# Projecting B and C of a state-space unit as one pair by seven quarter products

## The chip, the core and the metric

The kernel runs on one core of a Trainium2 chip, as one program in one launch. The metric is the device time in microseconds (us); the figure for a kernel is the median of its runs. All arithmetic is in float32.

The core has five engines, each of which works through its own queue of instructions in order: the Tensor engine (PE; its weight loads are listed apart as PEld), the Vector engine (DVE), the Scalar engine (ACT), the GpSimd engine (POOL) and the Sync engine (SP), which here only issues DMAs. An instruction that has to wait for another engine's result holds up everything behind it in its own queue.

## What is computed

The reference is a two-layer model over an input of 2 x 512 x 512. The change lies in the mixer of the second layer (`_L1_attn_ref`, a Mamba-2 block). Cut to what matters:

```python
proj = jnp.einsum('bsd,od->bso', h, in_proj_w)
gate = proj[..., :D_INNER]
hBC = proj[..., D_INNER:D_INNER + CONV_DIM]
hBC = jax.nn.silu(causal_conv(hBC, conv_w, conv_b))
hid = hBC[..., :D_INNER].reshape(b, s, H_M, P_M)
B = hBC[..., D_INNER:D_INNER + G_M * N_M].reshape(b, s, G_M, N_M)
C = hBC[..., D_INNER + G_M * N_M:].reshape(b, s, G_M, N_M)
...
M = jnp.einsum('bcihn,bcjhn->bcijh', Ch, Bh) * jnp.transpose(L, (0, 2, 3, 4, 1))
Y_diag = jnp.einsum('bcijh,bcjhp->bcihp', M, hc)
...
Y_off = jnp.einsum('bclhn,bchpn,bhcl->bclhp', Ch, prev_states, jnp.exp(A_cs))
y = (Y_diag + Y_off).reshape(b, S, H_M, P_M)[:, :s] + D_res
yg = y * jax.nn.silu(gate)
ygr = ygr * jax.lax.rsqrt(jnp.mean(ygr * ygr, axis=-1, keepdims=True) + EPS)
out = jnp.einsum('bsd,od->bso', y, out_proj_w)
```

Here the model width is 512 (four blocks of 128 rows, `KD` = 4), the sequence is 512 long (`S`; four chunks of 128, `NCH` = 4), there are 128 heads of 64 channels in 8 groups, and each group has one B and one C of 128 states for each of the two batch rows. B and C of one group and row are each the product of a 128 x 512 slice of the weight with the 512 x 512 input `hT`.

## The kernel before, in words

The mixer goes through 16 *units* (`u`), a group and a batch row each (`g, b = divmod(u, 2)`). A unit has 8 tiles of 128 channels, that is two heads each. They are taken two at a time by `step(d)`, so a unit has four steps, which are named by the number `t` of their first tile: t = 0, 2, 4, 6. In every step a pipeline is at work: `a` are the two tiles whose outputs are multiplied now, `n` the next two, whose decays, values and states are made ready, `h` the two after these, whose channels are projected, and `p` the previous two, whose outputs are gated, squared and summed.

Nothing is scheduled by a tool here. The whole stage is under `tc.manual_schedule()`, so each engine's queue has exactly the order in which `step` writes its instructions. Most steps go through the branch `if gates:`; the first unit and parts of the last take the `else` branch.

Names that the change and the prediction touch:

- `Values` and `Gates` project a pair of tiles (256 output columns) by *seven products of quarters*: the two factors are cut into quarters, sums of quarters are made beforehand (of the weight's by `row_sums`, four POOL instructions at L691; of the input's once, in `th`), and seven products in place of eight give the result after a few additions. `multiply(i)` writes product i; `product` (L717) is two matmuls over 128 rows with 256 columns. Products 1, 6, 7, 4 gather in one half of a PSUM bank, and in between its state is copied out by ACT (`copy`, L1464 and L1509) and added on by DVE (`add` and `add_fifth`, L1469, L1473, L1513).
- `project` (L1249) is the plain product: four matmuls over 128 rows with 512 columns.
- `inner(u, j)` projects B (j = 0) or C (j = 1) of a unit by `project` into the PSUM bank `of` (profile name `pjbc`). In step t = 0 of a unit it is done for the unit after it (`projected = u + 1`).
- `conv` is `first_tap` (ACT, L1259) and `taps` (three DVE instructions, L1268, each using the result of the one before). It is used for the channels (`hid`), for B (`BT`) and for C (`CT`).
- `clamp` (ACT, L1364, four instructions) and `decays` (an exponential on ACT into the single PSUM bank `de`, L1378, then a DVE product with `CB`, L1379) make the decay matrix of one head; there are two heads a tile, so four of these in each step.
- `values` (DVE, L1350) reads the transposed channels `px` (PE, L1340); `begun` (PE, `pn`, L1386), an ACT copy (L1395) and four DVE instructions (L1399) make the states `st`.
- `finish_y` (DVE, L1315 and L1316) takes a product `py` of the tiles `a` out of PSUM. `starts` (POOL, L1411) multiplies C into the decay tile `eb` that a DMA has brought.
- `square` (ACT, L1328) and its `add` (POOL, L1332) gather the squares of a unit; `squares` (PE, `ssq`, L1840) sums them over the partitions at the end of step t = 0 of the next unit. `root` (ACT with a table load, L1828) and a DVE reciprocal (L1829) follow in step t = 2.
- `Output` multiplies a finished unit by the output weights, again in seven products (`of`, `ofy`, L1640), in the steps t = 2, 4, 6 of the next unit; `added` is the DVE addition of a product to the result (L1663). The sums of quarters of y that it needs are made by POOL (L1608) into three rooms with the tags `s1`, `s2`, `s4`. In step t = 0 there is no output work.
- PSUM banks: `pj` has three buffers, `yy` two, `of`, `de` and `tr` one each.

In step t = 0 the order of the B and C work on PE was: products 1, 5, 2, 3 of the channels, then all of B, then the transposes of the second tile, the channels' product 6, and so on; C came in two halves of two matmuls, each between two products of the gates.

Of the kernel before, what the change touches and what calls it, by code (L numbers as in the profile page):

```python
# [8 lines left out]
F32 = mybir.dt.float32  # L9
# [6 lines left out]
P = 128  # L16
D = 512
B = 2
# [30 lines left out]
def fused_kernel(  # L49
# [1110 lines left out]
    with ExitStack() as sm:  # L1160
# [83 lines left out]
            sls[g] = wk.tile([P, 4, NT, GH], F32, tag="sl", name=f"sl{g}")  # L1244
            nc.sync.dma_start(sls[g], sl_d[g])

        def project(w_of, b, ps, ks=range(KD)):
            for k in ks:
                nc.tensor.matmul(  # L1249
                    ps, w_of(k), hT[:, k, bass.ts(b, S)], start=(k == 0), stop=(k == KD - 1)  # L1250
                )
# [84 lines left out]
        def transposed(s, spare=False):  # L1336
            tag, bufs = ("pj", 3) if spare else ("tr", 1)
            px = psum.tile([P, NCH, P], F32, tag=tag, name=f"px{s}", bufs=bufs)
            for c in range(NCH):
                nc.tensor.transpose(px[:, c, :], hid[s][:, bass.ts(c, P)], ident)  # L1340
            return px
# [67 lines left out]
        def starts(s):  # L1409

            nc.gpsimd.tensor_tensor(  # L1411
                eb_t[s],
                CTs[s // GT][:, P:].unsqueeze(1).to_broadcast([P, 2, S - P]),
                eb_t[s],
                ALU.mult,
            )
# [110 lines left out]
            project(lambda k: whs[s // 2][:, k, bass.ts(s % 2, P)], b, ps)  # L1527
            return ps, g * GT + t, hid[s]

        def inner(u, j, parts=False):  # L1530

            g, b = divmod(u, B)
            kept, name = ((BTs, "BT"), (CTs, "CT"))[j]
            kept[u] = wk.tile([P, S], F32, tag=name, name=f"{name}{u}", bufs=j + 1)
            if u == 0 and j == 1:
                ps = psum.tile([P, S], F32, tag="yy", name=f"pjbc{u}_{j}", bufs=2)
            else:
                ps = psum.tile([P, S], F32, tag="of", name=f"pjbc{u}_{j}")

            def go(ks):  # L1540
                project(lambda k: wbc[g][:, k, j, :], b, ps, ks)
                return ps, DIN // P + j * NG + g, kept[u]

            return go if parts else go(range(KD))

        def inner_products(u):

# [19 lines left out]
        class Output:  # L1567
# [18 lines left out]
            def banks(self, p):  # L1586

                return ("of", 1), ("yy", 2)
# [166 lines left out]
        def step(d):  # L1755
# [38 lines left out]
                    load_final(2 + i, sums_room(1, i))  # L1794


            for s in p:
                nc.gpsimd.tensor_tensor(y_of(s), y_of(s), sgs.pop(s), ALU.mult)  # L1798
            gates = ahead.pop(d, None)
            made = (g == 0 and b == 0 and t == 2) or (0 < g < NG and b == 1 and t == 0)  # L1800
            if (d - 1) in rest_of_sums:
                sum_out(g, 1)
# [51 lines left out]
            if gates:  # L1854

                def output(n=1):
                    if o:
                        o.multiply(n)

                def added():  # L1860
                    if o:
                        o.add()

                late = t == 2
                px = transposed(n[0])
                hids.multiply(1, 5)
                hcd = [values(n[0], px)]
                decays(n[0], 0)
                hids.copy(0, 0)
                hids.multiply(2, 3)  # L1870
                hids.add(0, 0)
                decays(n[0], 1)
                starts(n[0])
                output()
                if projected is not None:
                    b_of = inner(projected, 0)
                px = transposed(n[1])
                hids.multiply(6)
                if not late:
                    added()  # L1880
                hcd.append(values(n[1], px))
                decays(n[1], 0)
                if projected is not None:
                    conv(*b_of)
                hids.copy(0, 1)
                gates.multiply(1, 5)
                decays(n[1], 1)
                starts(n[1])
                if t == 4 and o:
                    o.sums(1)  # L1890
                hids.multiply(7)
                hids.copy(1, 1)
                gates.copy(0, 0)
                root()
                gates.multiply(2)
                pn = begun(n[0], hcd[0])
                hids.multiply(4)
                states(n[0], pn)
                if late:
                    added()  # L1900
                for f in [square(s) for s in p]:
                    f()
                hids.add_fifth()
                hids.add(0, 1)
                hids.add(1, 1)
                gates.multiply(6)
                output()
                if projected is not None:
                    c_of = inner(projected, 1, True)
                    c_of(range(0, KD // 2))  # L1910
                gates.copy(0, 1)
                convolved = hids.sum(0)
                first_tap(*convolved)
                if not late:
                    taps(*convolved, added)
                first_sums()
                gates.multiply(7)
                first_tap(*hids.sum(1))
                gates.copy(1, 1)

                def gates_added():
                    gates.add(0, 0)
                    gates.add(1, 1)

                if late:

                    def between():
                        added()
                        gates_added()


                    taps(*convolved, between)
                else:
                    gates_added()
                output()
                added()
                if projected is not None:
                    c_of = c_of(range(KD // 2, KD))
                pn = begun(n[1], hcd[1])
                gates.multiply(4)  # L1940
                taps(*hids.sum(1))
                output()
                added()
                states(n[1], pn)
                if projected is not None:
                    first_tap(*c_of)
                pss = squares()
                gates.multiply(3)
                silu()
                gates.add(0, 1)  # L1950
                output(int(t < 6))
                gates.silu()
                mean(pss)
                added()
                if projected is not None:

                    taps(*c_of)
# [206 lines left out]
```

## Time and profile before

| quantity | us |
|---|---|
| median of 3 runs | 2204.86 |
| lowest and highest run | 2204.32, 2205.11 |
| the profiled execution | 2207.44 |
| its span, first to last instruction | 2205.7 |
| a unit, from the first `py` product of one to that of the next (units 1 to 14) | 104.03 |
| of it the steps t = 0, 2, 4, 6 | 25.42, 26.52, 27.52, 24.57 |

The profile is of one execution. In a timeline row the columns are the start and the duration in us, the engine, the line of the kernel, the operation, what it writes and reads, the shapes and how many instructions are merged in the row; a bracket tells how long the engine was idle before it and what ended the wait. A matmul in float32 is two passes, so two matmuls are x4 there. Because matmuls overlap, the cost of a product is read from the start of its row to the start of the next, not from its duration. The granted clock of the Tensor engine is 0.996 over the span.

### The profile page before, as it was taken

How to read it: one execution, taken by the hardware profiler on the slowest of the kernel's cores; microseconds unless marked ns; L12 is line 12 of the kernel's file. 1: busy time of each engine (PE TensorE's matmuls, PEld its weight loads, DVE VectorE, ACT ScalarE, POOL GpSimd, SP SyncE). 2: the span in 40 equal slices, each digit the busy share in tenths (PEclk: the TensorE clock that was granted, in tenths of full speed). 3: DMA queues.
4: the chain of work that ended last, by engine and by line, in shares of the span. 5: the costliest groups of instructions: out<-in, count | busy, mean ns of one | idle time of the engine just before them, and what ended most of it. 6: DMA issues, size and time to landing. Idle time of an engine off the chain costs nothing.

```text
span 2205.7 us, 35586 instructions
## 1 busy us (share of the span) xinstructions
PE 2180.5 (99%) x12460; PEld 1704.9 (77%) x12460; DVE 1534.4 (70%) x3035; ACT 1295.2 (59%) x2878; POOL 1336.8 (61%) x1275
## 2 busy tenths in 40 slices
PE   8999999999999999999999999999999999999999
PEld 4545566865578888888888888888888888888877
DVE  6474577545877777777777677777777677777762
ACT  4231323215776767676767676767667676767661
POOL 4362532232556667766866586768567776766577
PEclk9999999999999999999999999999999999999999
DMA  5021466756544545443545554454446444544552
GB/s 169 20 77 38 139 220 214 253 171 208 169 144 131 156 139 173 125 134 125 179 137 153 158 154 125 134 163 130 145 140 193 132 137 125 167 126 139 150 177 93
DMA packets 196151, 323.21 MB, mean 147 GB/s; under 512 B 17795, under 2 KB 130180, under 8 KB 193540
## 3 DMA queue, kind: packets, MB, share of 16 engines
q1 hardware_dynamic: 189572, 299.95, 44.8%
q0 software_dynamic: 6400, 20.98, 2.5%
q8 instruction: 99, 1.62, 0.3%
q14 instruction: 80, 0.66, 0.1%
HBM read 294.12 MB, written 26.74 MB: 145 GB/s over the span
## 4 chain that ended last, share of the span: by engine, by line
PE 93%; DVE 3%; DMA 1%; ACT 1%; POOL 1%; issue 0%; SPq 0%; DVEq 0%; ACTq 0%; POOLq 0%
PE pjh L717 16%; PE of L1640 15%; PE gt L717 13%; PE py L1287 5%; PE pjbc L1249 5%; PE pf L1128 4%; PE py L1296 4%; PE pn L1386 4%; PE px L1340 3%; PE ofy L1640 3%; PE pg L717 2%; PE pu L717 2%; PE gty L717 2%; PE sh L610 2%; PE gt L1249 2%; PE pjh L1249 1%
## 5 line engine op out<-in xcount | busy, mean ns | idle before, releaser
L1411 POOL TENSOR_TENSOR eb<-CT,eb 128x768 f32<-128x768 f32 x128 | 230.4, 1820 | 350.1 <-DMA eb<-ea_d 317.4
L1364 ACT ACTIVATE cs<-cs,sl 128x128 f32<-128x128 f32 x1024 | 325.0, 390 | 0.6 <-DMA cs<-cs_d 0.6
L1268 DVE SCALAR_TENSOR_TENSOR hid<-pjh,cw,hid 128x511 f32<-128x511 f32 (+2 forms) x384 | 286.6, 747 | 42.0 <-ACT hid L1259 34.5
L1379 DVE TENSOR_TENSOR cs<-de,CB 128x512 f32<-128x512 f32 x256 | 175.5, 685 | 79.0 <-ACT de L1378 78.1
L1798 POOL TENSOR_TENSOR y<-y,sgt 128x512 f32<-128x512 f32 x124 | 177.0, 1447 | 12.7 <-ACT sgt L1520 10.1
L1287 PE MATMUL py<-cs,hc 128*64 128x128 f32 x2048 | 181.5, 277 | 0.0
L1332 POOL TENSOR_TENSOR sums<-sums,sq 128x512 f32<-128x512 f32 x110 | 139.8, 1271 | 60.0 <-ACT sq L1328 56.3
L1378 ACT ACTIVATE de<-cs 128x512 f32<-128x512 f32 x256 | 154.0, 602 | 30.5 <-DVE cs L1379 24.6
L1296 PE MATMUL py<-eb,st 128*64 128x128 f32 x1536 | 149.9, 274 | 0.0
L1399 DVE SCALAR_TENSOR_TENSOR st<-st,sl,pn 128x64 f32<-128x64 f32 x512 | 108.4, 275 | 59.4 <-ACT st L1395 59.4
L1663 DVE SCALAR_TENSOR_TENSOR acc<-of,rg,acc 128x256 f32<-128x256 f32 x188 | 90.2, 481 | 75.1 <-PE of L1640 74.8
L1464 ACT COPY hid<-pjh 128x256 f32<-128x256 f32 x171 | 63.6, 372 | 133.1 <-PE pjh L717 131.2
L1316 DVE SCALAR_TENSOR_TENSOR y<-hid,Dcol,y 128x512 f32<-128x512 f32 x128 | 135.7, 1060 | 4.5
L1287 PEld LDWEIGHTS py<-cs,hc 128*64 128x64 f32 x2048 | 122.5, 138 | 19.9 <-issue 18.1
L1315 DVE TENSOR_TENSOR y<-py,el 128x512 f32<-128x512 f32 x128 | 87.7, 685 | 58.5 <-PE py L1296 57.7
L1395 ACT COPY st<-pn 128x128 f32<-128x128 f32 x128 | 33.0, 263 | 153.3 <-PE pn L1386 153.3
L1640 PE MATMUL of<-wt,y 128*128 128x256 f32 x512 | 121.8, 381 | 0.0
L1249 PE MATMUL pjbc<-hT,wbc 128*128 128x512 f32 x256 | 119.5, 602 | 1.4 <-DVE g L1138 0.8
L1386 PEld LDWEIGHTS pn<-hcd,Bs 128*128 128x128 f32 x768 | 105.5, 192 | 18.5 <-issue 13.0
L1640 PE MATMUL of<-wo,s 128*128 128x256 f32 x496 | 118.8, 382 | 0.0
L717 PE MATMUL pjh<-th,sh 128*128 128x256 f32 x456 | 117.2, 379 | 0.0
L717 PE MATMUL pjh<-th,wh 128*128 128x256 f32 x456 | 117.2, 379 | 0.0
(389 smaller groups left out, 5534.0 us busy)
## 6 DMA issues: line engine op xcount, KB each, us to landing
cs<-cs_d SPq DMA_DIRECT2D x128, 512.0 KB, 4.3
eb<-ea_d SPq DMA_DIRECT2D x256, 192.0 KB, 6.1
wh<-in_in_wT SPq DMA_DIRECT2D x64, 512.0 KB, 9.2
wg<-in_in_wT SPq DMA_DIRECT2D x64, 512.0 KB, 7.5
el<-ea_d SPq DMA_DIRECT2D x256, 128.0 KB, 7.5
wo<-wo_d SPq DMA_DIRECT2D x16, 1024.0 KB, 8.3
wop<-in_out_wT SPq DMA_DIRECT2D x39, 256.0 KB, 2.8
wo_d<-wop POOLq DMA_DIRECT2D x39, 256.0 KB, 2.7
```

The source lines that it names most:

```text
L717: nc.tensor.matmul(ps, x[:, k, :], y[:, k, :], start=(first and k == 0), stop=(k == 1), skip_group_check=True,)
L1249: nc.tensor.matmul(ps, w_of(k), hT[:, k, bass.ts(b, S)], start=(k == 0), stop=(k == KD - 1))
L1268: nc.vector.scalar_tensor_tensor(dst[:, j:], ps[:, : S - j], cw[:, ct, KCONV - 1 - j : KCONV - j], dst[:, j:], ALU.mult, ALU.add,)
L1287: nc.tensor.matmul(py[bass.ts(hh, HP), bass.ts(c, P)], hc[:, c, bass.ts(hh, HP)], M[:, hh, bass.ts(c, P)], start=True, stop=(c == 0),)
L1296: nc.tensor.matmul(py[bass.ts(hh, HP), bass.ts(c, P)], st[:, c - 1, bass.ts(hh, HP)], cte[:, hh, bass.ts(c - 1, P)], start=False, stop=True,)
L1364: nc.scalar.activation(m[:, bass.ts(c, P)], m[:, bass.ts(c, P)], AF.Relu, bias=sls[g][:, 3, b * NCH + c, h0 + hh : h0 + hh + 1], scale=-1.0,)
L1378: nc.scalar.activation(pe, m, AF.Exp, scale=-1.0)
L1379: nc.vector.tensor_tensor(m, pe, CBs[s // GT].rearrange("p c i -> p (c i)"), ALU.mult)
L1386: nc.tensor.matmul(pn[:, c, :], Bss[s // GT][:, c, :], hcd[:, c, :], start=True, stop=True)
L1411: nc.gpsimd.tensor_tensor(eb_t[s], CTs[s // GT][:, P:].unsqueeze(1).to_broadcast([P, 2, S - P]), eb_t[s], ALU.mult,)
L1640: nc.tensor.matmul(ps, x[:, k, :], y[:, k, :], start=(first and k == 0), stop=(k == 3), skip_group_check=True,)
L1798: nc.gpsimd.tensor_tensor(y_of(s), y_of(s), sgs.pop(s), ALU.mult)
```

## The change

B and C of a unit are now projected together as a pair, like the channels, by seven products. A new class `Inner` does it:

```diff
+        class Inner:
+            def __init__(self, u):
+                self.u = u
+                self.g, self.b = divmod(u, B)
+                w = wbc[self.g].rearrange("p k j o -> p k (j o)")
+                room = [
+                    wk.tile([P, 4, P], F32, tag=f"s{i}", name=f"s{i}_bc{u}", bufs=1) for i in (1, 2, 4)
+                ]
+                s = [r[:, 2 * j : 2 * j + 2] for r in room[:2] for j in range(2)]
+                row_sums(w, *s)
+                self.factors = seven(w, s, hT[:, :, bass.ts(self.b, S)], self.b)
...
+            def banks(self):
+                self.ps = [
+                    psum.tile([P, 2, HD], F32, tag=tag, name=f"pjbc{self.u}_{j}", bufs=bufs)
+                    for j, (tag, bufs) in enumerate((("yy", 2), ("of", 1)))
+                ]
+            def multiply(self, *which):
+                for i in which:
+                    ps = self.ps[int(i not in (2, 3))][:, int(i in (3, 5))]
+                    product(ps, self.factors[i], i in (1, 2))
```

with `copy` (ACT), `add` and `add_fifth` (DVE) as in `Values`. The sums of the weight's quarters lie in the rooms `s1` and `s2` of the output's sums; B gathers in a `yy` bank, C in `of`. In step t = 0:

```diff
+            gates = ahead.pop(d, None)
+            if gates and projected is not None:
+                bc = Inner(projected)
             for s in p:
                 nc.gpsimd.tensor_tensor(y_of(s), y_of(s), sgs.pop(s), ALU.mult)
...
                 px = transposed(n[0])
+                if projected is not None:
+                    bc.banks()
+                    bc.multiply(1, 5)
+                    hids.multiply(1, 5)
+                    hcd = [values(n[0], px)]
+                    decays(n[0], 0)
+                    bc.copy(0, 0)
+                    bc.multiply(2, 3)
+                    clamp(n[0], 1)
+                    hids.copy(0, 0)
+                    bc.multiply(6)
+                    hids.multiply(2, 3)
+                    decays(n[0], 1, True)
+                    bc.add(0, 0)
+                    clamp(n[1], 0)
+                    bc.copy(0, 1)
+                    decays(n[1], 0, True)
+                    bc.add_fifth()
+                    bc.add(0, 1)
+                    first_tap(*bc.sum(0))
+                    hids.add(0, 0)
+                    starts(n[0])
+                    px = transposed(n[1])
+                    hids.multiply(6)
+                    hcd.append(values(n[1], px))
+                    taps(*bc.sum(0))
...
                 if projected is not None:
-                    c_of = inner(projected, 1, True)
-                    c_of(range(0, KD // 2))
+                    bc.multiply(7)
                 gates.copy(0, 1)
                 convolved = hids.sum(0)
                 first_tap(*convolved)
-                if not late:
+                if projected is not None:
+                    bc.copy(1, 1)
+                if not apart:
                     taps(*convolved, added)
                 first_sums()
                 gates.multiply(7)
...
+                if projected is not None:
+                    pn = begun(n[1], hcd[1])
+                    bc.multiply(4)
+                if apart:
                     def between():
                         added()
                         gates_added()
+                        if projected is not None:
+                            bc.add(1, 1)
                     taps(*convolved, between)
                 else:
                     gates_added()
...
-                if projected is not None:
-                    c_of = c_of(range(KD // 2, KD))
-                pn = begun(n[1], hcd[1])
+                if projected is None:
+                    pn = begun(n[1], hcd[1])
+                pss = squares()
                 gates.multiply(4)
...
                 if projected is not None:
-                    first_tap(*c_of)
-                pss = squares()
+                    first_tap(*bc.sum(1))
```

(`apart` is `late or projected is not None`, `late` is t = 2.) So in step t = 0 the additions of the gates, which stood behind all three taps of the first tile, now stand between its first and second tap; the three taps of B stand behind `values` of the second tile instead of behind its first decay; the sum of squares on PE stands ahead of the gates' product 4 instead of behind it; the POOL sums of the weight's quarters stand ahead of the gating of the previous two tiles. The first unit's own B and C, and those of unit 1, are still made by `inner`; the new way is taken in 14 steps, those with t = 0 of units 1 to 14. In steps t = 2, 4, 6 the order of the instructions is as before.

More of the change, by code (lines that the diff above doesn't have):

```diff
@@ L1245, in load_slice, with project @@
             nc.sync.dma_start(sls[g], sl_d[g])
-        def project(w_of, b, ps, ks=range(KD)):
-            for k in ks:
+        def project(w_of, b, ps):
+            for k in range(KD):
                 nc.tensor.matmul(
@@ L1528, in channels, with inner @@
             return ps, g * GT + t, hid[s]
-        def inner(u, j, parts=False):
+        def inner(u, j):
             g, b = divmod(u, B)
@@ L1538, in inner, with quarter, copy, add @@
                 ps = psum.tile([P, S], F32, tag="of", name=f"pjbc{u}_{j}")
[L1540 to L1544, printed above, removed]
+            project(lambda k: wbc[g][:, k, j, :], b, ps)
+            return ps, DIN // P + j * NG + g, kept[u]
+        class Inner:
[9 more added lines that the diff above has]
+                self.factors = seven(w, s, hT[:, :, bass.ts(self.b, S)], self.b)
+                self.kept = []
+                for j, (kept, name) in enumerate(((BTs, "BT"), (CTs, "CT"))):
+                    kept[u] = wk.tile([P, S], F32, tag=name, name=f"{name}{u}", bufs=j + 1)
+                    self.kept.append(kept[u])
+            def banks(self):
[7 more added lines that the diff above has]
+                    product(ps, self.factors[i], i in (1, 2))
+            def quarter(self, i, j):
+                return self.kept[i][:, bass.ts(j, HD)]
+            def copy(self, i, j):
+                nc.scalar.copy(self.quarter(i, j), self.ps[1][:, 0])
+            def add(self, i, j):
+                q = self.ps[i][:, j]
+                nc.vector.tensor_tensor(q, q, self.quarter(i, j), ALU.add)
+            def add_fifth(self):
+                q = self.quarter(0, 1)
+                nc.vector.tensor_tensor(q, self.ps[1][:, 1], q, ALU.add)
+            def sum(self, j):
+                ps = self.ps[j].rearrange("p i n -> p (i n)")
+                return ps, DIN // P + j * NG + self.g, self.kept[j]
         def inner_products(u):
@@ L1794, in step @@
                     load_final(2 + i, sums_room(1, i))
+            gates = ahead.pop(d, None)
+            if gates and projected is not None:
+                bc = Inner(projected)
             for s in p:
                 nc.gpsimd.tensor_tensor(y_of(s), y_of(s), sgs.pop(s), ALU.mult)
-            gates = ahead.pop(d, None)
             made = (g == 0 and b == 0 and t == 2) or (0 < g < NG and b == 1 and t == 0)
@@ L1864, in step @@
                 late = t == 2
+                apart = late or projected is not None
                 px = transposed(n[0])
[L1866 to L1874, printed above, removed]
-                if projected is not None:
-                    b_of = inner(projected, 0)
@@ L1877, in step @@
-                px = transposed(n[1])
-                hids.multiply(6)
-                if not late:
-                    added()
-                hcd.append(values(n[1], px))
-                decays(n[1], 0)
-                if projected is not None:
-                    conv(*b_of)
+                if projected is not None:
+                    bc.banks()
[23 more added lines that the diff above has]
+                    taps(*bc.sum(0))
+                else:
+                    hids.multiply(1, 5)
+                    hcd = [values(n[0], px)]
+                    decays(n[0], 0)
+                    hids.copy(0, 0)
+                    hids.multiply(2, 3)
+                    hids.add(0, 0)
+                    decays(n[0], 1)
+                    starts(n[0])
+                    output()
+                    px = transposed(n[1])
+                    hids.multiply(6)
+                    if not late:
+                        added()
+                    hcd.append(values(n[1], px))
+                    decays(n[1], 0)
@@ L1913, in step @@
                 first_tap(*convolved)
-                if not late:
+                if projected is not None:
+                    bc.copy(1, 1)
+                if not apart:
                     taps(*convolved, added)
@@ L1923, in gates_added @@
                     gates.add(1, 1)
-                if late:
+                if projected is not None:
+                    pn = begun(n[1], hcd[1])
+                    bc.multiply(4)
+                if apart:
                     def between():
@@ L1936, in step @@
                 added()
-                if projected is not None:
-                    c_of = c_of(range(KD // 2, KD))
-                pn = begun(n[1], hcd[1])
+                if projected is None:
+                    pn = begun(n[1], hcd[1])
+                pss = squares()
                 gates.multiply(4)
@@ L1955, in step @@
                 if projected is not None:
-                    taps(*c_of)
+                    taps(*bc.sum(1))
             else:
```

## The prediction

> **What bounds the kernel now.** I read the page's busy times first, then the busy time by stretches for the four steps of one unit, then the timelines of steps t = 0 and t = 2, each engine alone.
>
> ```profile
> span 2205.7 us, 35586 instructions
> PE 2180.5 (99%) x12460; PEld 1704.9 (77%) x12460; DVE 1534.4 (70%) x3035; ACT 1295.2 (59%) x2878; POOL 1336.8 (61%) x1275
> ```
> ```profile
> 942.03:967.45 25.42, 25.42 (x157) 19.65 (x156) 19.31 (x39) 17.66 (x40) 15.11 (x14) 1.00 0.47 135
> 967.46:993.98 26.52, 26.52 (x174) 23.15 (x173) 21.17 (x43) 21.21 (x48) 20.36 (x20) 1.00 0.49 150
> ```
>
> After the stretch and its length stand PE, PEld, DVE, ACT, POOL, granted clock, DMA share and GB/s. PE never rests: its matmuls follow one another through both steps of unit 4 at full clock, so a matmul less should be time less. But step t = 2 is the fullest for all four engines, and there the other queues run just in time. This is the step that the change doesn't edit, and the one that I think decides.
>
> Step t = 0, rows of ACT, PE, POOL and DVE:
>
> ```profile
> 947.66 0.37 ACT L1464 COPY hid<-pjh 128x256 f32<-128x256 f32 x1 [0.49 <-PE pjh L717]
> 948.33 1.03 PE L717 MATMUL pjh<-hT,sh 128*128 128x256 f32 x4
> 949.19 3.60 PE L1249 MATMUL pjbc<-hT,wbc 128*128 128x512 f32 x8
> 952.21 3.59 POOL L1411 TENSOR_TENSOR eb<-CT,eb 128x768 f32<-128x768 f32 x2 [3.75 <-DMA eb<-ea_d]
> 952.62 0.60 PE L1340 MATMUL px<-ident,hid 128*128 128x128 f32 x4
> 958.54 0.86 DVE L1399 SCALAR_TENSOR_TENSOR st<-st,sl,pn 128x64 f32<-128x64 f32 x4 [0.71 <-ACT st L1395]
> 961.06 2.32 DVE L1268 SCALAR_TENSOR_TENSOR hid<-pjh,cw,hid 128x511 f32<-128x511 f32 x3 [0.53 <-ACT hid L1259]
> 963.29 0.41 DVE L1513 TENSOR_TENSOR sgt<-sgt,gty 128x256 f32<-128x256 f32 x1
> 963.62 0.41 DVE L1513 TENSOR_TENSOR sgt<-sgt,gt 128x256 f32<-128x256 f32 x1
> 967.56 0.42 DVE L1513 TENSOR_TENSOR sgt<-sgt,gt 128x256 f32<-128x256 f32 x1 [0.54 <-PE gt L717]
> ```
>
> Step t = 2, rows of the same unit:
>
> ```profile
> 975.75 0.60 ACT L1378 ACTIVATE de<-cs 128x512 f32<-128x512 f32 x1 [1.11 <-DVE cs L1379]
> 979.68 0.60 ACT L1378 ACTIVATE de<-cs 128x512 f32<-128x512 f32 x1
> 980.43 0.37 ACT L1464 COPY hid<-pjh 128x256 f32<-128x256 f32 x1
> 982.63 0.18 DVE L1829 RECIPROCAL rg<-rg 128x4 f32<-128x4 f32 x1 [1.62 <-ACT rg L1828]
> 988.48 1.03 PE L717 MATMUL gt<-th,wg 128*128 128x256 f32 x4
> 988.84 0.48 DVE L1663 SCALAR_TENSOR_TENSOR acc<-of,rg,acc 128x256 f32<-128x256 f32 x1
> 989.37 1.99 PE L1640 MATMUL of<-wo,s 128*128 128x256 f32 x8
> ```
>
> The reader is to see the last two: the DVE addition ends at 988.84 + 0.48 = 989.32 and the output product behind it starts at 989.37. A product takes 0.863 to the next (948.33 to 949.19), so PE was free for it at 988.48 + 0.86 = 989.34. PE already arrives at this wait with nothing in hand.
>
> **What the change takes from PE.** The whole projection of B costs 952.62 - 949.19 = 3.43; C's two halves, from start to next start in the same timeline, 1.71 each. Together 6.86. Seven products at 0.863 are 6.04. The gain is 0.82 a unit, over 14 units 11.5 us. Moving `begun` and the sum of squares on PE changes their place and not their cost.
>
> **What it adds elsewhere.** ACT: three copies at 0.37 (row 947.66), 1.1 us; the first two replace waits for PE of 0.49 and more early in the step. DVE: four additions, 0.33 each start to start (963.29 to 963.62); three come before the middle of the step, where DVE sat idle 2.70 us for the transposes of the second tile, and cost nothing because of that idle time; without it they would cost 1.0. The fourth, for C, stands late, in a queue with no idle time, and costs its 0.33. POOL: four sums over 128 x 256, at 0.73 (the rows of `sh`), 2.92. They stand ahead of the gating, which ends 2.9 later, but the next POOL instruction waits for a DMA anyway: 3.75 idle in unit 4, 8.91 in unit 5. So nothing; if a DMA came sooner, they would cost up to 2.92 at the sum of squares, which waits for POOL's additions. Product 5 of the pair waits for the first sum: POOL turns from the gates' sums to the gating at 945.06 now, 3.03 after the step's start, so the first sum is there at 3.8; PE comes to product 5 one product after 945.74, at 4.6. No DMA is added or moved on a queue, and the PSUM bank `yy` that B takes was read by `finish_y` over 4 us before.
>
> **What it makes late.** In the old order one whole B (3.43) stood ahead of `begun` of the first tile; now products 1, 5, 2, 3, 6 of the pair do, 5 x 0.863 = 4.32. So `begun` comes 0.89 later, and with it the DVE states (958.54), three additions, ACT's first tap and the taps at 961.06. Behind these DVE has the same work as before plus the new addition (0.33), and a wait of about 0.13: the gates' additions now stand right behind the first tap and need ACT's copy, which comes behind two first taps and the new copy of C (0.68 + 0.27 + 0.68 + 0.37 after the start of the first of them; DVE's tap starts 0.83 after that, and DVE is free 1.08 later). Before, DVE waited 0.54 for PE at 967.56; that wait is used up. Sum: 0.89 + 0.33 + 0.13 - 0.54 = 0.81. DVE enters step t = 2 some 0.81 us later, while PE enters it 0.82 us earlier. The lag grows by 1.6.
>
> **Where the lag ends.** From 967.56 DVE works without a gap to the decay product that ACT waits for at 975.75 (1.11 idle). That exponential starts 0.81 later, and ACT goes through clamp, exponential, copy, clamp and exponential back to back until the one at 979.68, whose successor could start at 979.68 + 0.54 = 980.22. The copy at 980.43 waits for PE, so ACT has 0.21 in hand in unit 4. In unit 5 it has 0.47 (an exponential at 1083.45, the copy at 1084.46). PE is early, so this wait of ACT vanishes, and the copy comes 0.81 - 0.21 = 0.60 later than now in even units, 0.34 in odd ones. From there on I find no idle time up to 989.37: gate copy, table load, root, reciprocal (982.63), states, addition, three additions, first tap, taps, addition, output product. So PE's wait ends 0.60 and 0.34 later than it does now, and the rest of the step follows. PE's 0.82 are lost in standing still on the way, 1.42 and 1.16 a unit in step t = 2. In steps t = 4 and 6 PE's rows come from the same order; at the end of t = 2 DVE idles 1.05, so the lag ends there.
>
> **A term that I can't read off.** `finish_y`'s second instruction (L1316) takes 0.75 alone, longer when a POOL row meets it:
>
> ```profile
> 970.91 1.40 DVE L1316 SCALAR_TENSOR_TENSOR y<-hid,Dcol,y 128x512 f32<-128x512 f32 x1
> 972.95 1.04 DVE L1316 SCALAR_TENSOR_TENSOR y<-hid,Dcol,y 128x512 f32<-128x512 f32 x1
> 1074.94 0.84 DVE L1316 SCALAR_TENSOR_TENSOR y<-hid,Dcol,y 128x512 f32<-128x512 f32 x1
> 1076.42 1.30 DVE L1316 SCALAR_TENSOR_TENSOR y<-hid,Dcol,y 128x512 f32<-128x512 f32 x1
> ```
>
> The first two are unit 4's, the others unit 5's. Each ends about 0.55 after the POOL row that it met. Placed again by that, 0.8 later beside POOL rows that in even units shift with PE and in odd units stay (they hang on a DMA), the pair sums to 2.45 in even units (2.44 now) and to 1.95 in odd ones (2.14 now). So odd units lose 0.34 - 0.19 = 0.15. The ends: both alone, 1.50, or both as long as the worst in a step t = 0 or 2, 2.80. Even units then lie between 0.60 - 0.94 and 0.60 + 0.36, odd ones between 0.34 - 0.64 and 0.34 + 0.66: over 7 + 7 units -4.5 to +13.7 us.
>
> **The sum.** 7 x 0.60 + 7 x 0.15 = 5.3 us more. The profiled execution's span goes from 2205.7 to 2211.0; the median lies 0.8 below that span (2204.86), so I forecast 2210.
>
> The Trainium skill's "Perfetto Trace Analysis", section "Identifying the Most-Contended Engine", says to optimize the engine with the highest occupancy first. That is PE here, and by it alone the sum would be 2204.9 - 11.5 = 2193.4. The rows at 988.84 and 989.37 speak against it for this step.
>
> **Rivals.** (1) The gain is kept: the lag is absorbed ahead of the output product, and each unit saves its 0.82: 2193.4. For it: PE is 99% busy and DVE has 6 us of idle time in step t = 0. Against: that idle time lies ahead of `begun`, and the late part of the queue has none. It decides if DVE's lag stays under ACT's slack of 0.2 to 0.5. 0.13. (2) Give and take are about equal: L1316 meets POOL less, and the loss is near the gain: 2200.5 to 2209.2. 0.33. (3) A new stall inside step t = 0. The nearest are the sum of squares in odd units, where POOL's additions end at 1067.58 and PE would come at about 1067.96, 21.9 into a step of 24.6 (0.38 in hand, all hanging on a DMA), and the gates' product 7, whose start now comes two products, 1.73, behind that of product 6, while the copy that it waits for ends 1.07 + 0.37 = 1.44 behind it (958.91 and 959.98 now): 0.29 in hand. From the point where these are used up, each 0.5 us costs 7 us over 14 units: 2217 and more. 0.10. (4) The change doing less than it says: two of 16 units keep the old way, and that is in the sum.
>
> **How the numbers follow.** The forecast's own case, the gain lost and 0.3 to 0.9 more a unit on average, is 2209.2 to 2217, with a chance of 0.44. A difference under 0.2% (4.4 us) can't be told from no change here. Slower by more: this case and (3), 0.54. Within: (2), 0.33. Faster: (1), 0.13. The range takes in the low end of the L1316 bound and stops short of (1) and of most of (3): 2200 to 2216.
>
> **What would show it.** Right: in step t = 0 the pair's seven products in 6.0 and a step of 24.6; in step t = 2 PE idle or stretched by 1.0 to 1.5 us, mostly ahead of the transposes of the second tile, the channels' product 7 and the second-half output products, released by DVE L1350, ACT L1464 and DVE's addition; steps t = 4 and 6 at 27.5 and 24.6. Wrong: a step t = 2 still of 26.5 (then it is 2193), or PE waiting inside step t = 0.

## The result, and the profile after

The median rose from 2204.59 us to 2220.18 us: ratio 1.0074, 95% interval 1.0063 to 1.0085. The change made the kernel slower by 15.6 us. The forecast was 2210 with a range up to 2216; direction and place were right, the size was too small.

The busy times of the page of after, then the two steps of unit 4 by stretches (columns as before), then PE's waits (us in total, times, the longest):

```profile
span 2221.6 us, 36048 instructions
PE 2179.6 (98%) x12628; PEld 1737.3 (78%) x12628; DVE 1553.0 (70%) x3091; ACT 1305.9 (59%) x2920; POOL 1378.4 (62%) x1331
```
```profile
943.27:967.87 24.60, 24.60 (x170) 21.93 (x169) 18.81 (x37) 18.02 (x42) 17.95 (x18) 1.00 0.49 139
967.87:996.34 28.47, 27.11 (x173) 22.99 (x173) 23.39 (x50) 21.63 (x49) 20.33 (x20) 1.00 0.47 140
```
```profile
PE px L1340 <- DVE hcd L1350: 10.5, 12, 1.2
...
PE of L1683 <- DVE acc L1706: 5.1, 14, 0.4
```

The step that was edited is shorter, 24.60 against 25.42: PE has its 0.82 there, and it doesn't wait. The step behind it, with no edit, grew from 26.52 to 28.47, and PE rests in it (27.11 busy). PE's two new kinds of wait both end on DVE. The steps t = 4 and 6 stayed at 27.52 and 24.57. Units 1 to 14 together went from 1456.4 to 1471.0, so 14.6 of the 15.9 us between the two spans lie there: 1.13 in each even unit, 0.95 in an odd one on average.

DVE at the end of step t = 0 of unit 4, with the PE row of the pair's product 4 (it starts at 964.29):

```profile
960.67 0.86 DVE L1399 SCALAR_TENSOR_TENSOR st<-st,sl,pn 128x64 f32<-128x64 f32 x4 [0.85 <-ACT st L1395]
963.18 0.75 DVE L1268 SCALAR_TENSOR_TENSOR hid<-pjh,cw,hid 128x511 f32<-128x511 f32 x1 [0.53 <-ACT hid L1259]
963.85 0.41 DVE L1513 TENSOR_TENSOR sgt<-sgt,gty 128x256 f32<-128x256 f32 x1
964.46 0.42 DVE L1513 TENSOR_TENSOR sgt<-sgt,gt 128x256 f32<-128x256 f32 x1 [0.20 <-ACT sgt L1509]
965.36 0.43 DVE L1579 TENSOR_TENSOR pjbc<-pjbc,CT 128x256 f32<-128x256 f32 x1 [0.48 <-PE pjbc L717]
965.70 3.74 DVE L1268 SCALAR_TENSOR_TENSOR hid<-pjh,cw,hid 128x510 f32<-128x510 f32 x5
970.12 0.41 DVE L1513 TENSOR_TENSOR sgt<-sgt,gt 128x256 f32<-128x256 f32 x1
964.29 1.03 PE L717 MATMUL pjbc<-th,wbc 128*128 128x256 f32 x4
```

The new addition for C (L1579) is not only 0.33 of work: it waits 0.48 for product 4, which ends at 964.29 + 1.03 = 965.32. In the program product 4 is written ahead of the addition, and both touch the bank `of`, product 4 its first half and the addition its second, so the addition waits. The last gates' addition starts at 970.12, 26.85 into the step; before it was 967.56, 25.53 into a longer step. DVE is 1.32 late, not the 0.81 of the forecast.

Step t = 2 of the same unit:

```profile
978.35 0.60 ACT L1378 ACTIVATE de<-cs 128x512 f32<-128x512 f32 x1 [1.81 <-DVE cs L1379]
977.80 0.63 PE L1340 MATMUL px<-ident,hid 128*128 128x128 f32 x4 [0.89 <-DVE hcd L1350]
980.00 1.03 PE L717 MATMUL gt<-th,sw 128*128 128x256 f32 x4
981.13 1.13 PE L717 MATMUL pjh<-th,wh 128*128 128x256 f32 x4
990.35 1.03 PE L717 MATMUL gt<-th,wg 128*128 128x256 f32 x4
991.74 1.99 PE L1683 MATMUL of<-wo,s 128*128 128x256 f32 x8 [0.36 <-DVE acc L1706]
```

The lag surfaces where the forecast had put it: at the transposes of the second tile (0.89), at the channels' product 7 (981.13 - 980.00 is 1.13 where a product takes 0.86), and at the second-half output product (1.39 behind the gates' product; before, 0.89). Together 0.89 + 0.27 + 0.50 = 1.66 of the 1.95 by which the step grew. The other 0.29 is lost right at these waits: from start to start the first costs 1.06, and the products behind the first and the second start 0.02 and 0.10 later than they did.

### The profile page after: what moved, and what is told of

It is laid out like the page before. It is cut to its first block, busy times and chain, and to the rows that moved or that the text cites. A ratio compares the mean times of both kernels' runs of the same rounds, so it can differ in the third digit from the quotient of the medians.

```text
span 2221.6 us, 36048 instructions
## 1 busy us (share of the span) xinstructions
PE 2179.6 (98%) x12628; PEld 1737.3 (78%) x12628; DVE 1553.0 (70%) x3091; ACT 1305.9 (59%) x2920; POOL 1378.4 (62%) x1331
## 3 DMA queue, kind: packets, MB, share of 16 engines
q8 instruction: 100, 1.64, 0.3%
## 4 chain that ended last, share of the span: by engine, by line
PE 77%; DVE 13%; ACT 6%; issue 2%; DMA 1%; POOL 1%; SPq 0%; ACTq 0%; POOLq 0%; DVEq 0%
PE of L1683 13%; PE pjh L717 12%; PE gt L717 9%; PE py L1287 4%; PE pf L1128 4%; PE pjbc L717 4%; DVE hid L1268 4%; PE py L1296 3%; PE pn L1386 3%; PE pg L717 2%; PE pu L717 2%; PE px L1340 2%; PE gt L1249 2%; PE gty L717 2%; PE pjh L1249 2%
## 5 line engine op out<-in xcount | busy, mean ns | idle before, releaser
L1844 POOL TENSOR_TENSOR y<-y,sgt 128x512 f32<-128x512 f32 x124 | 161.4, 1323 | 21.6 <-ACT sgt L1520 18.9
L1316 DVE SCALAR_TENSOR_TENSOR y<-hid,Dcol,y 128x512 f32<-128x512 f32 x128 | 135.0, 1055 | 4.5
L717 PE MATMUL gt<-th,wg 128*128 128x256 f32 x456 | 118.3, 382 | 0.0
L717 PE MATMUL pjh<-hT,wh 128*128 128x256 f32 x456 | 117.1, 379 | 0.0
L717 PE MATMUL gt<-th,sw 128*128 128x256 f32 x456 | 117.0, 379 | 0.0
```

The source lines that it names most:

```text
L717: nc.tensor.matmul(ps, x[:, k, :], y[:, k, :], start=(first and k == 0), stop=(k == 1), skip_group_check=True,)
L1316: nc.vector.scalar_tensor_tensor(y, hid.pop(s), Dcol[:, ct : ct + 1], y, ALU.mult, ALU.add)
```

## The experiments

Nine kernels. The theories are named in the expectations: W, DVE's lag into t = 2 is what PE pays for, and the wait on product 4 is the missed part of it; P, the 0.89 of `begun`, or PE and its banks; X, L1316 against POOL. The steps are means over the seven even and seven odd units of the profiled execution; a ratio is to the runs of before that were made beside that kernel's.

| run | median us | ratio to before (95%) | t = 0 even, odd | t = 2 even, odd | units 1 to 14 |
|---|---|---|---|---|---|
| before | 2204.59 | | 25.42, 25.42 | 26.52, 26.52 | 1456.4 |
| after | 2220.18 | 1.0074 (1.0063 to 1.0085) | 24.60, 24.69 | 28.47, 28.21 | 1471.0 |
| c_addition_later | 2216.75 | 1.0046 (1.0032 to 1.0060) | 24.60, 24.60 | 28.30, 27.75 | 1466.0 |
| begun_early | 2230.09 | 1.0110 (1.0096 to 1.0124) | 25.20, 25.20 | 28.47, 28.23 | 1478.9 |
| both_and_gates | 2205.53 | 0.9995 (0.9984 to 1.0006) | 25.31, 25.31 | 26.52, 26.53 | 1454.9 |
| before_dve_late | 2228.30 | 1.0100 (1.0087 to 1.0114) | 25.42, 25.42 | 28.25, 28.05 | 1479.3 |
| all_and_pe_order | 2197.29 | 0.9959 (0.9944 to 0.9973) | 24.74, 24.74 | 26.51, 26.52 | 1446.8 |
| begun_early_2 | 2224.38 | 1.0081 (1.0067 to 1.0095) | 24.60, 24.75 | 28.47, 28.44 | 1473.1 |
| c_addition_first | 2214.85 | 1.0037 (1.0024 to 1.0049) | 24.86, 24.98 | 27.87, 27.43 | 1465.2 |
| before_dve_late_1 | 2205.53 (one run) | | 25.42, 25.42 | 26.52, 26.53 | 1456.6 |
| all_and_act_order | 2192.82 | 0.9945 (0.9932 to 0.9957) | 24.64, 24.65 | 26.52, 26.52 | 1445.6 |

**before_dve_late: lag without the change.** Before, with DVE work that nothing reads:

```diff
                 gates.add(0, 1)
+                if projected is not None:
+                    spare = wk.tile([P, 4, P], F32, tag="s4", name=f"spare{u}", bufs=1)
+                    spare = spare.rearrange("p k o -> p (k o)")[:, 0:HD]
+                    for _ in range(4):
+                        nc.vector.tensor_tensor(spare, gates.quarter(0, 1), gates.ps[:, 1], ALU.add)
```

> Before with four DVE additions more (the form of the gates' additions, 128 x 256 out of PSUM, written to a room that nothing reads) right behind the last gates' addition of t = 0, in 15 units. PE, ACT and POOL as before. It puts 4 x 0.33 = 1.32 of lag on DVE, the measure that after has. Theory W: PE's step t = 0 stays at 25.4, t = 2 grows by 1.32 - 0.21 = 1.1 in even units and by up to 1.32 - 0.47 = 0.85 in odd ones, 27.6 and 27.4; 14 units give 13.7: 2218. Theory P (PE or its banks, and not DVE's lag, make t = 2 long in after): little, 2205 to 2208.

Nothing of the pair is in this kernel, and yet t = 2 grows from 26.5 to 28.2, with PE's waits at the same instructions as in after. Stretches and two PE rows of unit 4's step t = 2:

```profile
967.62:995.83 28.21, 27.11 (x173) 23.01 (x173) 22.96 (x47) 21.15 (x48) 20.29 (x20) 1.00 0.49 141
```
```profile
977.29 0.63 PE L1340 MATMUL px<-ident,hid 128*128 128x128 f32 x4 [0.62 <-DVE hcd L1350]
991.23 1.99 PE L1640 MATMUL of<-wo,s 128*128 128x256 f32 x8 [0.37 <-DVE acc L1663]
```

So DVE's lag alone is enough to make what after shows; PE's banks or the pair's products are not needed for it. The size was missed because the four additions took 0.45 each and not 0.33: C's taps ended 1.82 later. ACT's second exponential in t = 2 came 1.93 later in unit 4 and the step lost 1.69, so ACT had 0.24 in hand there (0.21 in the forecast).

**before_dve_late_1: one such addition.**

> Before with one DVE addition more behind the last gates' addition of t = 0, in place of four. The four took 0.45 each, start to start, and DVE came 1.82 later into t = 2, where the even units lost 1.69. Theory W with a slack of ACT of 0.21: lag 0.46, L1316 as before, even units' t = 2 at 26.52 + 0.46 - 0.21 = 26.77; odd ones, with 0.47 in hand, at 26.5. A straight line without slack: 26.52 + 0.46 x 1.69 / 1.82 = 26.95 in even units.

Nothing was lost in even units, against both forms of the expectation. C's taps end 0.45 later, but the first L1316 behind them, DVE and then POOL's gating of the same unit:

```profile
969.11 0.96 DVE L1316 SCALAR_TENSOR_TENSOR y<-hid,Dcol,y 128x512 f32<-128x512 f32 x1
970.71 1.05 DVE L1316 SCALAR_TENSOR_TENSOR y<-hid,Dcol,y 128x512 f32<-128x512 f32 x1
968.23 2.98 POOL L1798 TENSOR_TENSOR y<-y,sgt 128x512 f32<-128x512 f32 x2
```

It took 0.96 where it took 1.40 before, and ended 4.88 into the step (4.85 before). L1316 ends with a POOL row, not 0.75 after its own start: the second one ends at 971.76, POOL's gating at 971.21, 0.55 earlier. So a small lag is swallowed here, as long as L1316 meets the same POOL row as before and is longer than the 0.75 that it takes alone.

**c_addition_later: the wait on product 4 taken away on DVE.** From here on every kernel is after with an edit.

```diff
                         gates_added()
-                        if projected is not None:
-                            bc.add(1, 1)
                     taps(*convolved, between)
+                    if projected is not None:
+                        bc.add(1, 1)
```

> After with one DVE instruction moved: the addition for C stands behind all three taps of the channels' first tile instead of between the first and the second. In the profile of after it waits 0.48 us for product 4 of the pair, which fills the other half of the same bank. Theory W (DVE is late into t = 2, and this wait is the part that the forecast missed): the wait goes, DVE's last gates' addition starts 26.85 - 0.48 = 26.4 us into the step t = 0, t = 2 of even units takes 28.47 - 0.48 = 28.0, and 14 units give 6.7: 2213.5. Theory P (the loss comes from begun being late by 0.89, or from PE and its banks): the addition waits or not, t = 2 stays at 28.5, 2220. Theory X (L1316 meets POOL longer): no step change, within 2 us of 2220, and the L1316 pair changes.

The addition no longer waits and DVE's last gates' addition starts at 26.28, as W says. But even units' t = 2 got only 0.17 of it. C's addition now ends 0.87 later than in after, and with it ACT's first tap of C; so the silus behind that on ACT, and POOL's gating, gain little, and L1316 ends with the gating:

```profile
971.19 1.83 DVE L1316 SCALAR_TENSOR_TENSOR y<-hid,Dcol,y 128x512 f32<-128x512 f32 x1
969.98 2.50 POOL L1844 TENSOR_TENSOR y<-y,sgt 128x512 f32<-128x512 f32 x2 [0.73 <-ACT sgt L1520]
```

POOL ends at 972.48, L1316 at 973.02. The same rows of after, and the gating of before:

```profile
973.46 1.44 DVE L1316 SCALAR_TENSOR_TENSOR y<-hid,Dcol,y 128x512 f32<-128x512 f32 x1
971.85 2.50 POOL L1844 TENSOR_TENSOR y<-y,sgt 128x512 f32<-128x512 f32 x2 [0.91 <-ACT sgt L1520]
970.49 2.95 POOL L1798 TENSOR_TENSOR y<-y,sgt 128x512 f32<-128x512 f32 x2
```

Counted from the start of t = 0, DVE's end of C's taps came 0.57 earlier than in after, POOL's gating only 0.16.

The same count shows what happened in after itself. The gating starts there at 28.58 and before at 28.46, so it hardly moved, while DVE's end of C's taps came 1.31 later. The first L1316 slid from the first gating instruction, behind which it ends 0.55 later in before, to the second: 971.85 + 2.50 = 974.35, and L1316 ends at 974.90. In unit 4 of c_addition_later and of c_addition_first, with 0.75 and 0.76 of DVE's lag left, it still ends behind the second; in before_dve_late_1, with 0.46, behind the first. That is why a part of the lag, taken out alone, gave back so little here.

**c_addition_first: the same wait turned round.** DVE's order stays as in after; product 4 follows the addition on PE:

```diff
                     pn = begun(n[1], hcd[1])
-                    bc.multiply(4)
...
                 pss = squares()
+                if projected is not None:
+                    bc.multiply(4)
                 gates.multiply(4)
```

> After with one PE instruction group moved: product 4 of the pair stands behind the addition for C and behind the sum of squares, so that PE waits for DVE (some 0.1) and DVE no longer for PE (0.48). The addition for C keeps its place on DVE, between the channels' first and second tap, so that ACT's first tap of C, and with it ACT's silus and POOL's gating in t = 2, don't slide back by 0.8 as in c_addition_later, where POOL's gating came only 0.16 earlier and the first L1316 grew from 1.44 to 1.83. Theory W + POOL (an L1316 that meets a POOL row ends 0.55 after the end of that row; so the lag counts only if the gating moves along): DVE's last gates' addition at 26.85 - 0.48 = 26.4 into t = 0 and the gating some 0.45 earlier, the first L1316 of even units at 1.44 again, t = 2 there 28.47 - 0.48 = 28.0. Odd units may lose up to 0.5 in t = 0 where POOL's additions of squares end later than 21.0 into the step. 2212 to 2216. Theory W without POOL's part: the same as c_addition_later, t = 2 at 28.3 in even units.

The DVE row of the addition, L1316 and the gating:

```profile
962.78 0.43 DVE L1579 TENSOR_TENSOR pjbc<-pjbc,CT 128x256 f32<-128x256 f32 x1
...
970.89 1.64 DVE L1316 SCALAR_TENSOR_TENSOR y<-hid,Dcol,y 128x512 f32<-128x512 f32 x1
969.48 2.50 POOL L1844 TENSOR_TENSOR y<-y,sgt 128x512 f32<-128x512 f32 x2 [0.27 <-ACT sgt L1520]
```

The addition starts without a wait, at the same place in DVE's queue. Even units' t = 2 fell by 0.60, to 27.87. But 0.26 of this is only PE entering the step later: it paid that in t = 0, where product 4 came 1.08 behind the sum of squares instead of the 0.81 that this takes otherwise. Both steps together are 0.34 shorter than in after. That is twice the 0.17 of c_addition_later and short of the 0.48 of W with POOL's part, so the run lies between the two forms of W. By the units it is 5.8 us less than after, c_addition_later 5.0: taken away in two ways, the wait on product 4 is shown to be a part of the loss. L1316 took 1.64 and not 1.44 again, because the gating moved by 0.35 and DVE by 0.56.

**begun_early and begun_early_2: the 0.89 alone.**

```diff
                 if t == 4 and o:
                     o.sums(1)
+                if projected is not None:
+                    states(n[0], begun(n[0], hcd[0]))
                 hids.multiply(7)
```

with the old `begun` and `states` left to the other steps; `begun_early` also puts ACT's first tap ahead of the gates' copy (0, 1).

> After with begun and the states of the first tile ahead of the channels' product 7, and ACT's first tap ahead of its gates' copy. This takes away DVE's wait of 0.85 for the states, more or less the 0.89 by which the forecast had begun late. Theory W: no gain, because the addition for C still waits for product 4, which ends at the same time (22.05 into the step) whatever came before: its wait grows from 0.48 to some 1.3, t = 2 stays at 28.5 in even units, 2220. Theory P (the 0.89 is what DVE carries into t = 2): 14 x 0.85 = 11.9 less, 2208, t = 2 at 27.6.

> As the run begun_early, but ACT's gates' copy stays ahead of its first tap (there the copy stood behind it and PE waited 0.3 for it). Theory W: t = 0 takes 24.60 again, the addition for C still ends with product 4, so t = 2 stays at 28.5 in even units and the time at that of after, 2217 to 2222. Theory P (the 0.89 of begun is what DVE carries): t = 2 at 27.6, 2208.

t = 2 stayed at 28.47 in even units in both: that `begun` comes late is not by itself what costs the time. In begun_early_2 the states' wait of 0.85 is gone, but waits of 0.65 on the channels' product 4 and 0.73 on ACT's first tap come behind it, and the first tap on DVE stands at 963.21 in unit 4, 19.91 into the step exactly as in after. W's reason was only half of it: besides product 4 of the pair, ACT's gates' copy, which waits for PE's product 6, holds the same queue. In begun_early my exchange on ACT made a new stall, which no theory had: PE waited for the gates' copy in each of 14 units, and t = 0 took 25.20.

```profile
963.22 1.13 PE L717 MATMUL gt<-th,wg 128*128 128x256 f32 x4 [0.33 <-ACT sgt L1509]
```

**both_and_gates: all the late waits at once.** Besides the edits of begun_early:

```diff
                 hids.add(1, 1)
+                if projected is not None:
+                    gates.add(0, 0)
...
                     pn = begun(n[1], hcd[1])
-                    bc.multiply(4)
-                if apart:
+                    taps(*convolved, lambda: None, lambda: bc.add(1, 1))
+                    gates.add(1, 1)
+                    bc.multiply(4)
+                elif apart:
```

(`taps` got a second function to call ahead of its third instruction, and ACT's copy of C moved behind both first taps.)

> After with begun and states early as in the run before, the gates' first addition ahead of the first tap, the second behind the third tap, and the addition for C between the second and third tap, recorded ahead of product 4, so that PE waits for DVE there and not DVE for PE. All the work of after is done. Theory W: the waits of 0.85, 0.20, 0.48 and most of 0.53 go, DVE's last gates' addition starts about 24.8 into a step of 24.6 (25.5 into a step of 25.4 before), so the lag of before is there again: t = 2 at 26.5 to 26.7, the 0.82 a unit of PE is kept, 2204.6 - 11.5 = 2193, at most 2196. If begun and the addition for C merely added up: 2220 - 11.9 - 6.7 = 2202. Theory P with the cause in PE's banks: t = 2 stays above 28, 2210 or more.

t = 2 is 26.52 again in every unit: with DVE's lag gone (last gates' addition 0.15 behind the start of t = 2, 0.11 before) so is the whole loss of t = 2. An early `begun` and a free addition for C, which alone had given 0 and 0.17 in even units, gave 1.95 together with the moved additions of the gates. t = 0 is 25.31 for the same 0.33 wait of PE as in begun_early, which was expected nowhere.

**all_and_pe_order, all_and_act_order: the stall in t = 0 taken out.** First the channels' product 4 is recorded behind DVE's additions and the pair's product 7; then ACT's gates' copy (0, 0) goes ahead of the channels' copy (1, 1).

```diff
                 if projected is not None:
                     bc.multiply(7)
+                    hids.multiply(4)
```
```diff
-                hids.copy(1, 1)
+                if projected is None:
+                    hids.copy(1, 1)
                 gates.copy(0, 0)
+                if projected is not None:
+                    hids.copy(1, 1)
```

> As the run both_and_gates, with two places changed: ACT's copy of the gates (0, 1) comes behind the first tap as there, but the first tap no longer waits long, because the channels' product 4 is recorded behind the channels' DVE additions and stands on PE behind the pair's product 7 (in both_and_gates DVE's first of these additions waited 0.64 for product 4, and PE waited 0.33 for ACT's gates' copy behind the first tap and restarted twice 0.1 slower). Theory W (DVE's lag and in-order waits are all there is): t = 0 comes back from 25.31 to 24.60 with DVE's last gates' addition at about 24.7, t = 2 stays at 26.52, a unit takes 103.2, 14 x 0.82 = 11.5 less than before: 2193.5. Rival (moving the lag out only shifts the stall; t = 0 and t = 2 can't both be short): t = 0 or t = 2 keeps 0.4 or more of the loss, 2199 or more.

> As all_and_pe_order, with two copies of ACT exchanged: the gates' copy (0, 0) ahead of the channels' copy (1, 1). In all_and_pe_order the gates' product 6 started 0.14 late, right behind the end of the gates' copy, which stood behind the copy that waits for the channels' product 7. Theory W: t = 0 goes from 24.74 to 24.60, t = 2 stays at 26.52, 14 x 0.14 = 2.0 less: 2195 against 2197.3, a unit at 103.2. Rival: the channels' copy comes later by 0.27 and product 4 or the taps wait for it, no gain: 2197 or more.

Stretches of unit 4 in the second:

```profile
934.32:958.96 24.64, 24.64 (x169) 21.85 (x168) 20.66 (x43) 18.75 (x43) 17.98 (x18) 1.00 0.45 139
958.96:985.48 26.52, 26.52 (x173) 23.15 (x172) 21.28 (x44) 21.09 (x48) 20.38 (x20) 1.00 0.52 150
```

Both steps are short, a unit takes 103.25, and PE doesn't wait. All the arithmetic of after is done, only the order differs. It beats both kernels, 2192.82 with a ratio of 0.9945 to before; of the first step's 0.14 above 24.60, 0.10 came back, 1.3 us over the units (2.0 expected).

## Why the prediction was wrong

*What bounds, and PE's gain.* Right: t = 0 took 24.60, and the loss fell in t = 2.

*What is covered.* Right for ACT's copies, the three early additions and POOL's sums. The earlier place of the sum of squares on PE was not free in units 11 and 13: there it waited for POOL's additions, ahead of which POOL had stood idle 6.50 and 6.60 for a DMA, and t = 0 took 24.86 and 24.96. That is the place of rival 3. No cost of it shows: these units took 104.61 and 104.64, unit 7 without that wait 104.61. The gates' product 7 did not wait.

*What is late: the failed step.* "The fourth, for C, stands late, in a queue with no idle time, and costs its 0.33", beside "a wait of about 0.13". The wait measured 0.20, and the addition cost 0.34 and a wait of 0.48, because I had let it depend on ACT's copy alone and not on product 4, which is recorded ahead of it in the same bank. By the rows: 0.88 + 0.34 + 0.20 + 0.48 - 0.54 = 1.36, measured 1.32 at the gates' addition and 1.31 at the end of C's taps. c_addition_first, where the addition runs without the wait, shows the term. The 0.88 is the forecast's 0.89 and right in size, but `begun` is not alone in holding it: in begun_early_2 the channels' product 4 and ACT's gates' copy kept the first tap at the same 19.91.

The Trainium skill's "PSUM — Partial Sum Buffer", section "PSUM bank collisions raise a hardware error", says that two engines may not be in one bank and quadrant at once, even in different columns. No run here tries that. What the runs show is that the two could change places, and that this was worth 5.8 us.

*Where the lag ends.* Right: ACT's slack was 0.24 (0.21), and from there the lag was PE's loss. In unit 4 of after the second exponential came 2.19 later into t = 2 than before (10.48 against 8.29), and the step grew by 1.95.

*L1316.* Even units right, 2.49 (2.45). Odd units were put at 1.95 and measured 1.94 to 2.81, on average 2.31. The forecast had read unit 5 alone for them, 2.14; before, the seven odd units already took 2.01 to 2.46.

*The sum.* 5.3 was forecast, the units lost 14.6. The lag's missing 1.31 - 0.81 = 0.50 is 7.0 over 14 units; the other 2.3 lie almost wholly in odd units, where L1316 was the term that came out longer. Without the wait, in c_addition_first, the kernel measured 2214.85, inside the range. The spans differ by 1.3 more outside units 1 to 14. The range stopped at 2216 because it carried bounds for L1316 alone: the lag was given as one number, without bounds.

*Rivals.* The gain kept (1) needed a lag under ACT's slack; it had 1.32, and came true in all_and_act_order once the lag was out. Rival (2) asked for a shorter L1316, and it came out longer. The Trainium skill's "Perfetto Trace Analysis", section "Identifying the Most-Contended Engine", says to optimize the engine with the highest occupancy first, where the Tensor engine's headroom is to be judged by its FLOP rate and its weight loads; these were 77% busy here, still more than any other engine. By that rule alone the estimate was 2193.4. The change as it was made measured 2220.18, and 2192.82 came out only when DVE's and ACT's queues were put in order too.

## What to carry to other kernels

Where in-order queues meet just in time, work saved on the busiest engine is worth only what the lag of the others into the next stage leaves of it: add up the lag of each engine, and for each added instruction ask for every earlier writer of the same bank or tile, not only for its operands. Take late waits out together: one alone mostly uncovers the next, on DVE, on ACT or through POOL. When an engine's order is changed to help another, look first at what the exchanged instruction was holding up.

## What the runs showed of the hardware

The first two L1316 of a step t = 2, whose two large inputs lie in SBUF, ended 0.55 us after the end of a POOL instruction that they met in 299 of 308 cases (units 1 to 14 of the eleven profiles), whether that instruction still had 0.20 or 1.30 to run when they started; they took 0.75 to 1.85. The other nine took 0.75: eight met one with less than 0.20 left, and one began 0.07 ahead of one. A POOL instruction behind could be stretched in turn, from 1.27 to 1.72 or from 0.73 to 1.18. The Trainium skill's "SBUF — State Buffer", section "Terms", describes a shared port pair that one of the two engines holds for a whole instruction while the other blocks; the ends agree with it, but no run here tells the port from another cause. The lag of 0.45 that vanished in before_dve_late_1 follows from these ends.

A product for which PE waited 0.27 or more lasted 1.13 instead of 1.03, and the next one started 0.97 behind it instead of 0.86: such a wait costs PE 0.1 on top. DVE additions that read or write what the one before them wrote stood 0.45 apart, the others 0.33.

Near the end of the run the granted clock of PE dropped to 0.50 for a few us, differently from profile to profile: from 2108.1 to 2111.5 before, from 2120.0 to 2126.8 in after. So the same step t = 2 of the last unit took 28.18 at a mean of 0.94 before and 29.32 at 0.90 after; in before_dve_late it took 27.86 at 1.00, and 0.80 of that was waiting. In the profile of after the last unit and the tail took 3.7 us longer than before, and what lies ahead of unit 1 took 2.4 less; that is the 1.3 outside units 1 to 14. What makes the clock drop there stays open.
